# Graph attention layer on one NeuronCore: nodes laid out in 49 blocks of 128 where there were 50, node tables computed in 7 pieces of 7 blocks where there were 5 of 10

## The chip, the cores and the metric

The kernel runs on one core of one Trainium2 chip. The metric is the device time of one execution in microseconds. Three runs of the kernel before took 2503.68, 2481.40 and 2481.17 us; the median is 2481.4 us.

## The reference

6250 nodes with 64 features, 206,250 edges (100,000 random pairs in both directions, 200,000 in all, and one loop for each node), sorted by destination. For each edge the keys of its source, the queries of its destination and a projected edge feature are multiplied and summed in 4 heads of 16; the score is clipped to -5..5 and exponentiated, weighs the source's value row, and the messages are summed per destination. The sum is added to the node's features, and each row is normalized.

```
Kh = (x @ Wk.T + bk).reshape(n, H, D)
Qh = (x @ Wq.T + bq).reshape(n, H, D)
Vh = (x @ Wv.T + bv).reshape(n, H, D)
Ee = (edge_attr @ We.T + be).reshape(-1, H, D)
score = (Kh[src] * Qh[dst] * (1.0 / np.sqrt(D)) * Ee).sum(-1)
score = jnp.exp(jnp.clip(score, -5.0, 5.0))
msg = Vh[src] * score[..., None]
wV = jax.ops.segment_sum(msg, dst, num_segments=n)
out = _layernorm(x + wV.reshape(n, H * D))
```

## The kernel before

*Layout.* The nodes are padded to `NR = 128 * NB` rows, with `NB = 50`: 6400. Node n is row `n // NB` and block `n % NB` of a tile with 128 partitions. The edges are cut into 1612 tiles of 128 edges (`T`), eight tiles make a group (`G`), so there are 202 groups. Two groups make a step (the last steps have one); there are 105 steps.

*Start (before the main loop).* xT, with a row of ones, is loaded in `NB // CB` pieces of `CB = 10` blocks, by the ACT and SP queues in turn (L215, the ones by DVE in L216). For each piece the key and value rows of its blocks are computed by a matmul per block (L331), evicted two blocks at a time by ACT (L333), and written to the table `kv_tab` in HBM (L334). A second pass over the pieces does the queries (L361): ACT rounds them to bf16 (L363), DVE takes the remainder (L364), and a middle and a low part follow one pair of blocks later (L351 and L352, `rest_of_q`); each piece is written to `q3_tab` (L371) as three bf16 parts. Meanwhile POOL gathers the rows of x for the first 32 tiles (L238), and later, once `kv_tab` and the edges' sources `src_i` are there, the first key and value rows (L446). Last, the node features themselves are turned, split into three bf16 parts, and kept in SBUF as `parts`, one 128 x 192 tile for each of the `NB` blocks (L404 to L415).

*Where an edge gets its key and value row.* Of the 16 tiles of a step, 14 are gathered from `kv_tab` by POOL, one indirect DMA for each tile (L446). Five buffers of a step's size exist (`KVB`), and the gather for a later step waits until DVE's message (L617) has read the buffer. The other two tiles of most steps are *picked*: for a batch of 4 tiles (512 edges, two steps) the feature rows of the sources are made by one-hot matmuls over all node blocks. ACT computes `src - NB * row` (L493, `from`), DVE compares it with the block numbers (L503, `hots`), which gives for each block a 128 x 512 one-hot in bf16, and PE multiplies the block's `parts` with it: the high and middle parts (L514) and the low part (L519). When all blocks of a batch are summed, ACT copies the two results out (L526, L527), PE applies the key and value weights (L530 to L535, `picked_kv`), and ACT places the rows in the buffer (L541, `place_kv`).

*One batch in the main loop.* There are 47 such batches, and a batch spans four groups, g = 4m + i with i = 0 to 3. `CUTS` cuts the blocks into pieces of at most `MOST` blocks; a piece is one L503 instruction and one buffer of the pool `hot` (7 buffers). `PIECES` says which pieces go with which i. Before: 14 blocks in four pieces at i = 0, and 12 blocks in three pieces at i = 1, 2 and 3.

*Order in a group.* The program is written out by hand, engine by engine in this order: loads by SP (edges L175, queries L189, keys L554); DVE's products of this group (L600, L601, L604, L606); the first piece of the next group's one-hots (L503); DVE's add of a finished step (L644); the copies L526 and L527 (i = 0 alone); the picks of this group on PE (for i = 0 they stand after the following PE work); the edge projection for the next group (L435, onto a bias that ACT wrote in L564); the sums of a step (L630, 32 matmul passes, at every second group); the queries of the group after the next (L594); `picked_kv` (i = 0 and 2); on ACT the destination one-hots (L571, L577), `from` (L493), a widening copy (L625), `place_kv` (L541, i = 1 and 3), the bias (L564) and the exponential of the score (L610); DVE's message for the group before (L617); POOL's gathers; DVE's edge one-hots (L585); and the remaining pieces of the next group's one-hots (L503). Finished node blocks are closed, normalized and written out on the way (L658 to L679).

Of the kernel before, what the change touches and what calls it, by code (L numbers as in the profile page):

```python
# [7 lines left out]
F32 = mybir.dt.float32  # L8
BF16 = mybir.dt.bfloat16
I32 = mybir.dt.int32  # L10
AF = mybir.ActivationFunctionType
# [3 lines left out]
P = 128  # L15
N = 6250
C = 64
# [9 lines left out]
NR2 = 112  # L27
LG = 2
RG = 16
NB = 50  # L30
NR = P * NB
RING = 8
STEP = 31
# [1 line left out]
BATCHES = 16, 32, 47  # L35
KEYS = 26 * 8
W = 42
CB = 10
KVB = 5
XG = 4  # L40
TB = 4
# [21 lines left out]
AHEAD = 3  # L63
BATCH = 4
LAST = (NS - 8 - AHEAD) // 2
CUTS = 0, 4, 8, 12, 14, 18, 22, 26, 30, 34, 38, 42, 46, 50
MOST = 4
PIECES = (0, 1, 2, 3), (4, 5, 6), (7, 8, 9), (10, 11, 12)


def place_of(g):
# [36 lines left out]
def tile_gnn(ctx: ExitStack, tc: tile.TileContext, x, xT, wT, bias, beT, weT, eT, src, src_rows, dst,  # L108
             dst_rows, out):
    nc = tc.nc  # L110
    consts = ctx.enter_context(tc.tile_pool(name="consts", bufs=1))
    dram = ctx.enter_context(tc.tile_pool(name="dram", bufs=1, space=bass.MemoryType.DRAM))
# [1 line left out]


    kv_tab = dram.tile([NR, 2 * C], F32, name="kv_tab")
    q3_tab = dram.tile([NR, 3 * C], BF16, name="q3_tab")
    key_tab = dram.tile([NR2, 2 * G * P], BF16, name="key_tab")
    kv_v = kv_tab.rearrange("(p b) c -> p b c", p=P)
    q3_v = q3_tab.rearrange("(p b) (i c) -> p b i c", p=P, i=3)  # L120

    src_i = consts.tile([P, T], I32, name="src_i")
    dst_i = consts.tile([P, T], I32, name="dst_i")
# [37 lines left out]
    bkv_p = consts.tile([3, 2, 2 * C], BF16, name="bkv_p")  # L161
    parts = consts.tile([P, NB + 1, 3, C], BF16, name="parts")
    parts_flat = parts.rearrange("p b i c -> p (b i c)")
# [27 lines left out]
    with tc.tile_pool(name="nodes", bufs=1) as nodes, \  # L191
# [20 lines left out]
        rows_i = nodes.tile([NR2, 2, G * P], I32, name="rows_i")  # L212
        for i in range(NB // CB):
            s = slice(i * CB * P, (i + 1) * CB * P)
            (nc.scalar, nc.sync)[i % 2].dma_start(xT_sb[:C, s], xT[:, s])  # L215
# [41 lines left out]
        nc.vector.tensor_scalar(minus_row3, row3, -1.0, None, op0=OP.mult)  # L257
        nc.vector.tensor_scalar(minus_row50, row, -float(NB), None, op0=OP.mult)
        nc.vector.tensor_copy(row_b, row_i)
# [5 lines left out]
        def three_parts(out_, values, n, times):  # L265

            part = nodes.tile([3, n], BF16, name="part", bufs=2)
            mask = nodes.tile([3, 1], F32, name="mask", bufs=2)
            cut = nodes.tile([3, n], F32, name="cut", bufs=2)
            nc.vector.memset(cut, 0.0)  # L270
            for i in range(3):
                nc.vector.tensor_copy(part, values)
                nc.vector.tensor_scalar(mask, row[:3], float(i), None, op0=OP.is_equal)
                nc.vector.scalar_tensor_tensor(cut, part, mask, cut, op0=OP.mult, op1=OP.add)
                if i < 2:
                    nc.vector.tensor_sub(values, values, part)
            nc.vector.tensor_copy(out_, cut[:, None, :].to_broadcast([3, times, n]))

        def weights():
# [3 lines left out]
            nc.vector.tensor_scalar(bkv_sb[:, :C], bkv_sb[:, :C], 1.0 / D ** 0.5, None, op0=OP.mult)  # L283
            nc.vector.memset(parts[:, NB, 0], 0.0)

# [36 lines left out]

        q3 = nodes.tile([P, NB, 3, C], BF16, name="q3")
        for i in range(NB // CB):
            bs = slice(i * CB, (i + 1) * CB)
            kv_sb = chunks.tile([P, CB, 2 * C], F32, name="kv_sb")
            for b in range(0, CB, 2):
                ps = npsum.tile([P, 2, 2 * C], F32, name="ps")
                for u in range(2):
                    c0 = (i * CB + b + u) * P  # L330
                    nc.tensor.matmul(ps[:, u, :], xT_sb[:, c0:c0 + P], w_sb[:, :2 * C], start=True,  # L331
                                     stop=True)
                nc.scalar.activation(kv_sb[:, b:b + 2, :], ps, AF.Copy)  # L333
            nc.sync.dma_start(kv_v[:, bs, :], kv_sb)  # L334
            if i == 0:
                nc.sync.dma_start(rows_i, dst_rows)
# [10 lines left out]
        late = []  # L347

        def rest_of_q():
            q, two = late.pop(0)  # L350
            nc.scalar.activation(q3[:, two, 1], q, AF.Copy)  # L351
            nc.vector.tensor_sub(q3[:, two, 2], q, q3[:, two, 1])  # L352

        for i in range(NB // CB):
            for b in range(0, CB, 2):
                two = slice(i * CB + b, i * CB + b + 2)
                ps = npsum.tile([P, 2, 2 * C], F32, name="ps")
                q = ps[:, :, :C]
                for u in range(2):
                    c0 = (i * CB + b + u) * P  # L360
                    nc.tensor.matmul(q[:, u, :], xT_sb[:, c0:c0 + P], w_sb[:, 2 * C:], start=True,  # L361
                                     stop=True)
                nc.scalar.activation(q3[:, two, 0], q, AF.Copy)  # L363
                nc.vector.tensor_sub(q, q, q3[:, two, 0])  # L364
                late.append((q, two))
                if len(late) > 1:
                    rest_of_q()
            if late and b == CB - 2:
                rest_of_q()
            bs = slice(i * CB, (i + 1) * CB)  # L370
            nc.sync.dma_start(q3_v[:, bs], q3[:, bs])  # L371
        three_parts(be_p, be_sb, C, G)
        three_parts(bkv_p, bkv_sb, 2 * C, 2)
        masks()
# [82 lines left out]
    with tc.If(rv == 0) as branch:  # L457

        with tc.tile_pool(name="work", bufs=2) as work, \
# [3 lines left out]
            TO, OH, OF, PE, PQ, MSG, KB, SCORE, HOT, FROM, SRC = ({} for _ in range(11))  # L463
# [16 lines left out]
            def pairs(ap):  # L480

                return ap.rearrange("p (a b) -> p a b", b=2)
# [12 lines left out]
            def pieces(g):  # L495

                return [(g // 4, c) for c in PIECES[g % 4]] if 0 <= g < 4 * LAST else []

            def hots(m, c):
                lo, hi = CUTS[c], CUTS[c + 1]  # L500
                HOT[m, c] = work.tile([P, MOST, BATCH * P], BF16, name="hot", bufs=7)
                shape = [P, hi - lo, BATCH * P // 2, 2]
                nc.vector.tensor_tensor(  # L503
                    HOT[m, c][:, :hi - lo].rearrange("p b (a c) -> p b a c", c=2),
                    pairs(FROM[m])[:, None].to_broadcast(shape),
                    block2[:, lo:hi, None, :].to_broadcast(shape), op=OP.is_equal)

            def picks(todo):

                blocks = [(b, HOT[mc][:, b - CUTS[mc[1]], :]) for mc in todo  # L510
                          for b in range(CUTS[mc[1]], CUTS[mc[1] + 1])]
                for b, hot in blocks:
# [188 lines left out]
            for mc in pieces(0):  # L701
                hots(*mc)
            for g in range(NG + 1):
                now, before = g < NG, g > 0
                i, m = g % 4, g // 4
# [12 lines left out]
                for mc in ahead[:1]:  # L718
                    hots(*mc)
# [42 lines left out]
                for mc in ahead[1:]:  # L762
                    hots(*mc)
# [196 lines left out]
```

## Time and profile before

| what | value |
|---|---|
| runs | 2503.68, 2481.40, 2481.17 us; median 2481.4 us |
| profiled execution | 2496.53 us, its span 2494.6 us |
| granted TensorE clock, mean | 0.825 |
| PE busy | 1935.9 us (78%) in 12,299 matmul passes |
| DVE busy | 1494.2 us (60%) |
| POOL busy | 1350.8 us (54%), of it 1319.3 us in 1392 gathers |
| ACT busy | 908.6 us (36%) |
| picks, L514 and L519 | 583.8 + 306.1 us busy, 2350 matmuls each |
| one-hots, L503 | 697.2 us, 611 instructions |
| HBM | 218.74 MB read, 7.79 MB written |

Lines of the profile read as: line of the kernel, engine, operation, result <- operands, shapes, count; then busy time, mean duration, and the idle time of the engine just ahead of such instructions with what ended it ("issue" where the profile shows nothing that the engine waited for, "remote" where the releaser can't be told). PEld is the loading of weights. Timeline lines begin with the start and the duration in us from the start of the span.

### The profile page before, as it was taken

What the parts mean: (1) busy time and instruction counts of PE and PEld (TensorE: products, weight loads), DVE (VectorE), ACT (ScalarE), POOL (GpSimd) and SP (SyncE); (2) the same over time, 40 slices, a digit from 0 to 9 for tenths busy, and PEclk for the clock granted to TensorE, in tenths of its full rate; (3) what the DMA queues carried; (4) which work ended last, traced back from release to release, by engine and by line L of the source; (5) the groups of instructions that cost most, each with busy time, mean ns of one, the idle gap of its engine ahead of it and who ended that gap; (6) DMA issues with size and microseconds to landing.
All of it is one profiled execution on the core that took longest, in us unless ns stands there. A gap on an engine that the chain in (4) does not pass through costs nothing. (4 is left out here: it accounts for less than half of the span.)

```text
span 2494.6 us, 32642 instructions
## 1 busy us (share of the span) xinstructions
PE 1935.9 (78%) x12299; PEld 1331.1 (53%) x12299; DVE 1494.2 (60%) x2314; ACT 908.6 (36%) x1268; POOL 1350.8 (54%) x1434
## 2 busy tenths in 40 slices
PE   4477887887887887877778788788788778788875
PEld 4435555555555555455555555555555555455574
DVE  2356665665666666666556566566666666666653
ACT  1242433433442434233424234233343343342452
POOL 5435555555555555555555555555555555555551
PEclk9978888887887888788788788788888788888865
DMA  4332333333332333333323233233333332332341
GB/s 119 125 96 77 100 91 86 99 97 82 99 97 80 98 91 104 87 83 97 95 82 92 79 101 98 78 99 90 91 103 86 88 101 79 95 93 83 87 114 25
DMA packets 140877, 228.84 MB, mean 92 GB/s; under 512 B 71126, under 2 KB 71576, under 8 KB 140598
## 3 DMA queue, kind: packets, MB, share of 16 engines
q1 hardware_dynamic: 94758, 133.30, 18.3%
q0 software_dynamic: 45568, 92.37, 14.2%
q8 instruction: 98, 1.61, 0.3%
q10 hardware_dynamic: 384, 1.00, 0.2%
q14 instruction: 69, 0.57, 0.1%
HBM read 218.74 MB, written 7.79 MB: 91 GB/s over the span
## 5 line engine op out<-in xcount | busy, mean ns | idle before, releaser
L446 POOL DMA_INDIRECT kv<-kv_tab,src_i x1392 | 1319.3, 948 | 1086.1 <-DVE msg L617 642.3
L503 DVE TENSOR_TENSOR hot<-from,still 128x2048 bf16<-128x2048 bf16 (+1 forms) x611 | 697.2, 1173 | 156.9 <-PE low L519 117.0
L630 PE MATMUL room<-msg,off 128*128 128x64 f32 x3224 | 498.3, 298 | 284.8 <-issue 277.4
L630 PEld LDWEIGHTS room<-msg,off 128*128 128x128 f32 x3224 | 472.9, 220 | 304.3 <-issue 296.0
L514 PE MATMUL pick<-hot,parts 128*128 128x512 bf16 x2350 | 583.8, 401 | 9.3 <-issue 9.0
L541 ACT ACTIVATE kv<-room 128x256 f32<-128x256 f32 x94 | 36.2, 385 | 1379.0 <-PE room L630 511.8
L514 PEld LDWEIGHTS <-parts 128*128 128x128 bf16 x2350 | 235.7, 103 | 299.1 <-issue 88.7
L601 DVE TENSOR_TENSOR prod<-prod,pe 128x512 f32<-128x512 f32 x202 | 138.8, 687 | 418.4 <-remote 323.7
L435 PE MATMUL pe<-we_sb,et 128*128 128x128 f32 x1612 | 292.0, 331 | 110.5 <-ACT pe L564 68.9
L435 PEld LDWEIGHTS pe<-we_sb,et 128*128 128x128 f32 x1612 | 243.3, 229 | 182.7 <-ACT pe L564 88.9
L519 PE MATMUL low<-hot,parts 128*64 128x512 bf16 x2350 | 306.1, 386 | 14.5 <-issue 13.8
L577 ACT ACTIVATE to<-to,one_p 126x1024 bf16<-126x1024 bf16 x202 | 232.0, 1148 | 6.6
L571 ACT ACTIVATE to<-kb,minus_row 126x1024 bf16<-126x1024 bf16 x202 | 230.0, 1139 | 10.9 <-remote 5.5
L519 PEld LDWEIGHTS <-parts 128*64 128x64 bf16 x2350 | 120.3, 110 | 190.0 <-issue 114.8
L625 ACT ACTIVATE off<-of 128x2048 f32<-128x2048 bf16 (+2 forms) x105 | 191.9, 1828 | 52.5 <-remote 20.8
L644 DVE SCALAR_TENSOR_TENSOR acc<-room,above,acc 128x64 f32<-128x64 f32 x103 | 29.0, 282 | 243.2 <-ACT kv L541 177.9
L600 DVE TENSOR_TENSOR prod<-kv,pq 128x512 f32<-128x512 f32 x202 | 137.5, 681 | 25.2 <-remote 6.8
L594 PE MATMUL pq<-qw,to 126*128 126x64 bf16 x1612 | 109.7, 217 | 50.4 <-issue 40.2
L617 DVE TENSOR_TENSOR msg<-kv,score 128x512 f32<-128x512 f32 x202 | 138.7, 687 | 16.9 <-ACT score L610 12.7
L604 DVE TENSOR_REDUCE score<-prod 128x32 f32<-128x512 f32 x202 | 138.3, 685 | 6.9
L594 PEld LDWEIGHTS <-to 126*128 126x128 bf16 x1612 | 103.4, 120 | 61.1 <-issue 56.5
L585 DVE TENSOR_TENSOR of<-still,key 128x2048 bf16<-128x2048 bf16 (+2 forms) x105 | 123.3, 1175 | 0.2
(122 smaller groups left out, 1050.1 us busy)
## 6 DMA issues: line engine op xcount, KB each, us to landing
et<-in_eT SPq DMA_DIRECT2D x100, 512.0 KB
kb<-key_tab SPq DMA_DIRECT2D x201, 252.0 KB
kv<-kv_tab,src_i POOLq DMA_INDIRECT x1392
srcs<-in_src_rows SPq DMA_DIRECT2D x47, 256.0 KB
qw<-q_tab SPq DMA_DIRECT2D x202, 15.8 KB
kv_tab<-kv_sb SPq DMA_DIRECT2D x5, 640.0 KB
q_tab<-q SPq DMA_DIRECT2D x5, 480.0 KB
acc<-in_x SPq DMA_DIRECT2D x48, 32.0 KB
```

The costliest lines, as they stand in the source:

```text
L435: nc.tensor.matmul(pe[:, 2 * u:2 * u + 2, :], et[:, u, :], we_sb, start=False, stop=u == n // 2 - 1, skip_group_check=True)
L446: nc.gpsimd.indirect_dma_start(out=kv_of(g)[:, j, :], out_offset=None, in_=kv_tab[:, :], in_offset=bass.IndirectOffsetOnAxis(ap=src_i[:, t ...
L503: nc.vector.tensor_tensor(HOT[m, c][:, :hi - lo].rearrange("p b (a c) -> p b a c", c=2), pairs(FROM[m])[:, None].to_broadcast(shape), bloc ...
L514: nc.tensor.matmul(hi_mid, parts_flat[:, at:at + 2 * C], hot, start=b == 0, stop=b == NB - 1)
L519: nc.tensor.matmul(low[u * C:(u + 1) * C], parts_flat[:, at:at + C], hot, start=b < 2, stop=b >= NB - 2, skip_group_check=True)
L571: nc.scalar.activation(TO[g][:, :n, :], KB.pop(g)[:, :n * P].rearrange("p (j e) -> p j e", j=n), AF.Square, bias=minus_row3[:3 * W])
L577: nc.scalar.activation(TO[g][:, :n, :], TO[g][:, :n, :], AF.Relu, bias=one_p[:3 * W], scale=-1.0)
L594: nc.tensor.matmul(PQ[g][:, j, :], TO[g][:, j, :], QW[g], start=j == 0, stop=j == n - 1, skip_group_check=True)
L601: nc.vector.tensor_mul(prod[:, :n, :], prod[:, :n, :], PE[g][:, :n, :])
L617: nc.vector.tensor_mul(MSG[s][:, k:k + n, :].rearrange("p g (h d) -> p g h d", h=H), kv_of(g)[:, :n, C:].rearrange("p g (h d) -> p g h d", ...
L625: nc.scalar.activation(OF[s][:, :n, :], OH.pop(s)[:, :n, :], AF.Copy)
L630: nc.tensor.matmul(pa, OF[s][:, j, :], MSG[s][:, j, :], start=j == 0, stop=j == n - 1)
```

## The change

The nodes are laid out in 49 blocks (6272 rows). The tables are computed in 7 pieces of 7 blocks; since 7 is odd, each piece has three pairs of blocks and a single one, in both passes. A batch's blocks are cut into 12 pieces, eleven of 4 blocks and a last one of 5, three at each i; so the blocks at i = 0 to 3 are 12, 12, 12 and 13. The one-hot tiles hold 5 blocks each, and their pool has 6 buffers. A query window may reach beyond the last node, so `q3_tab` gets 64 more rows, which are filled by one more DMA.

```diff
-NB = 50
+NB = 49
-CB = 10
+CB = 7
-CUTS = 0, 4, 8, 12, 14, 18, 22, 26, 30, 34, 38, 42, 46, 50
-MOST = 4
-PIECES = (0, 1, 2, 3), (4, 5, 6), (7, 8, 9), (10, 11, 12)
+CUTS = 0, 4, 8, 12, 16, 20, 24, 28, 32, 36, 40, 44, 49
+MOST = 5
+PIECES = (0, 1, 2), (3, 4, 5), (6, 7, 8), (9, 10, 11)
...
-    q3_tab = dram.tile([NR, 3 * C], BF16, name="q3_tab")
+    q3_tab = dram.tile([NR + 64, 3 * C], BF16, name="q3_tab")
-    q3_v = q3_tab.rearrange("(p b) (i c) -> p b i c", p=P, i=3)
+    q3_v = q3_tab[:NR, :].rearrange("(p b) (i c) -> p b i c", p=P, i=3)
...
             for b in range(0, CB, 2):
-                ps = npsum.tile([P, 2, 2 * C], F32, name="ps")
-                for u in range(2):
+                n = min(2, CB - b)
+                ps = npsum.tile([P, 2, 2 * C], F32, name="ps")[:, :n]
+                for u in range(n):
...
-                nc.scalar.activation(kv_sb[:, b:b + 2, :], ps, AF.Copy)
+                nc.scalar.activation(kv_sb[:, b:b + n, :], ps, AF.Copy)
...
-                two = slice(i * CB + b, i * CB + b + 2)
+                n = min(2, CB - b)
+                two = slice(i * CB + b, i * CB + b + n)
                 ps = npsum.tile([P, 2, 2 * C], F32, name="ps")
-                q = ps[:, :, :C]
-                for u in range(2):
+                q = ps[:, :n, :C]
+                for u in range(n):
...
-            if late and b == CB - 2:
+            if late and b + 2 >= CB:
                 rest_of_q()
...
             nc.sync.dma_start(q3_v[:, bs], q3[:, bs])
+            if i == 0:
+                nc.sync.dma_start(q3_tab[NR:, :], q3[:64, 0].rearrange("p i c -> p (i c)"))
...
-                HOT[m, c] = work.tile([P, MOST, BATCH * P], BF16, name="hot", bufs=7)
+                HOT[m, c] = work.tile([P, MOST, BATCH * P], BF16, name="hot", bufs=6)
```

## The prediction

> **What bounds the kernel now.** I read the page first (who is busy), then the timelines of all engines through one batch, then a table of windows over the same batch, and last the start.
>
> ```profile
> PE 1935.9 (78%) x12299; PEld 1331.1 (53%) x12299; DVE 1494.2 (60%) x2314; ACT 908.6 (36%) x1268; POOL 1350.8 (54%) x1434
> L446 POOL DMA_INDIRECT kv<-kv_tab,src_i x1392 | 1319.3, 948 | 1086.1 <-DVE msg L617 642.3
> L514 PE MATMUL pick<-hot,parts 128*128 128x512 bf16 x2350 | 583.8, 401 | 9.3 <-issue 9.0
> L519 PE MATMUL low<-hot,parts 128*64 128x512 bf16 x2350 | 306.1, 386 | 14.5 <-issue 13.8
> ```
>
> No engine is full. The picks are the largest single work of PE, 583.8 + 306.1 = 890 us for 2350 blocks, 0.379 us a block. But 559 us of the span PE is idle, so the question is where in a batch that idle time lies. A batch (four groups, i = 0 to 3) is marked by the L526 copies: 47 of them from 188.3 to 2373.6, so 2185.3 / 46 = 47.5 us each. I take the batch from 1386.3 to 1433.96. Its windows (columns: busy time and count of PE, PEld, DVE, ACT, POOL, granted clock, DMA share, GB/s):
>
> ```profile
> 1386.30:1397.60 11.30, 11.26 (x60) 6.96 (x61) 6.86 (x11) 7.92 (x10) 5.67 (x6) 0.74 0.53 154
> 1397.60:1408.50 10.90, 10.90 (x87) 7.26 (x86) 8.02 (x12) 0.00 (x0) 7.75 (x8) 1.00 0.17 44
> 1408.50:1418.40 9.90, 9.56 (x72) 6.00 (x68) 8.89 (x15) 8.45 (x11) 5.98 (x7) 1.00 0.57 152
> 1418.40:1430.40 12.00, 3.76 (x15) 2.94 (x15) 3.75 (x5) 0.00 (x0) 7.26 (x8) 0.68 0.19 50
> 1430.40:1434.00 3.60, 3.04 (x20) 2.90 (x20) 3.16 (x6) 0.96 (x4) 0.00 (x0) 0.50 0.00 0
> ```
>
> PE is full for 32 us, then does 15 matmuls in 12 us, then works at half clock. The PE timeline says where:
>
> ```profile
> 1390.96 3.74 PE L514 MATMUL pick<-hot,parts 128*128 128x512 bf16 x14
> 1394.63 1.70 PE L519 MATMUL low<-hot,parts 128*64 128x512 bf16 x14
> 1396.26 2.76 PE L514 MATMUL pick<-hot,parts 128*128 128x512 bf16 x12
> 1398.96 1.49 PE L519 MATMUL low<-hot,parts 128*64 128x512 bf16 x12
> 1412.48 2.75 PE L514 MATMUL pick<-hot,parts 128*128 128x512 bf16 x12
> 1417.58 1.00 PE L630 MATMUL room<-msg,off 128*128 128x64 f32 x7
> 1426.86 0.27 PE L630 MATMUL room<-msg,off 128*128 128x64 f32 x1 [1.43 <-issue]
> 1430.42 2.58 PE L630 MATMUL room<-msg,off 128*128 128x64 f32 x11 [0.47 <-issue]
> ```
>
> After seven of the 32 sums of i = 3 the matmuls come one or two at a time, 0.7 us and its multiples apart, with no releaser ("issue"), until 1430.4. Beside it stands POOL, whose gathers come 1.25 us apart in runs of 6, 8 and 14 in this batch:
>
> ```profile
> 1398.58 1.13 POOL L446 DMA_INDIRECT kv<-kv_tab,src_i  x1 [3.48 <-DVE key_i L441]
> 1408.57 0.39 ACT L541 ACTIVATE kv<-room 128x256 f32<-128x256 f32 x1 [14.28 <-PE low L519]
> 1409.62 0.69 DVE L617 TENSOR_TENSOR msg<-kv,score 128x512 f32<-128x512 f32 x1 [0.16 <-issue]
> 1410.59 0.94 POOL L446 DMA_INDIRECT kv<-kv_tab,src_i  x1 [2.12 <-DVE msg L617]
> ```
>
> The run of 14 goes from 1410.59 to 1427.80, and the stall from 7.8 us after its start to 2.6 us after its end. Nearly every other long run does the same (first gap 7.8 to 10.6 us in); runs of 6 show none. ACT is held as well: L541 waits only for matmuls of groups before, yet starts at the end of the run of 8 (1398.58 to 1408.46). It lets the L564 bias, the exponential, the L617 message and so the run of 14 go. So a batch is PE's work plus a stall of some 12 us that POOL's runs place.
>
> **The change, part by part.** A block costs 2.76 / 12 + 1.49 / 12 = 0.354 us on a warm PE. The blocks of a batch go from 14, 12, 12, 12 to 12, 12, 12, 13.
>
> *Picks of i = 0, two blocks fewer:* -0.71 us. They lie before the runs of 8 and 14. PE next needs another engine at the edges L435 in i = 2 (1409.96), which need the ACT bias L564 that ended at 1409.45. If ACT stays where POOL's run puts it, PE can come at most 0.51 us earlier here, some 0.3 us in batches where L541 came later (L541 at 23.1 us of the batch in most, at 21.2 to 22.2 in others). Bounds 0 to 0.71; I take 0.5, the middle of the two caps and the whole.
>
> *Picks of i = 3, one block more:* +0.354 us. They lie in the 7.8 us before the stall, so three sums (0.11 us each) move behind it. At the half clock there they cost 0.22 each, so 0.35 to 0.66. I take 0.35: where the run of 14 and its stall begin 1.3 us earlier, batches are equally long (46.5, 46.9, 47.1 us against 46.3, 46.6, 47.3), so work pushed past the stall costs its own length.
>
> Net -0.15 us a batch (bounds -0.36 and +0.66), by 47: **-7 us** (-17 to +31).
>
> By the Trainium skill, "TensorE: Matmul & The Clock Gate", Part 1, the array runs at half rate after an idle window and is released after some 3.4 us of activity; were both removed blocks cold, i = 0 would be relieved of 1.06 us instead. The trace agrees on the gate (0.50 granted from 1430.4, 1.00 from 1397.6), and the 3.74 us for 14 against 2.76 for 12 shows the late ones warm, so the sum keeps 0.71.
>
> *Merged runs.* In 295.9, 1095.0, 1668.0, 1856.0 and 2142.7 (batch starts) L541 came before 21 us, the run of 8 ran into the next 6, and the batch took 48.6 to 49.2 us against about 46.8: +2.0 us. There the sums of i = 1 ended 4.6 to 5.1 us after the run of 8 began; in most others 6 to 7.3, in six 5.6 to 5.9. The run of 8 mostly begins at 11.7 to 11.8 us of the batch whether the lows of i = 0 ended at 9.0 or 10.5, so with fewer picks it stays, and the sums come up to 0.71 earlier: the six fall to about 5.0. Bounds 0 and 20 more merged batches (+40 us); I take four, **+8 us**.
>
> *One-hots:* per batch 13 L503 instructions (12 of 1.21 us, one of 0.68) become 12, the last 1.21 x 5/4 = 1.5 us: 0.4 us less DVE work. DVE idles 0.2 to 8 us ahead of its products for PE, which hides it: 0. The 0.3 us more stand before the L617 message of i = 3, needed at the seventh gather of the run (1418.09); it ended at 1417.55, so 0.5 us cover it; without cover 14 us in all, kept in the range. Six hot buffers instead of seven: a piece now reuses that of two groups before, whose lows precede on PE the edges that DVE's products wait for. Only i = 1 has no such cover, and there both versions wait for the same piece. 0.
>
> *Start.* 25 evictions of the kv table become 28, one block fewer; likewise for q (two ACT copies and two DVE subtractions each). While POOL gathers, ACT gets one through in some 9 us:
>
> ```profile
> 40.96 0.39 ACT L333 ACTIVATE kv_sb<-ps 128x256 f32<-128x256 f32 x1 [10.11 <-remote]
> 65.40 0.95 POOL L446 DMA_INDIRECT kv<-kv_tab,src_i  x1 [22.73 <-DMA src_i<-in_src]
> 106.18 0.28 ACT L363 ACTIVATE q<-ps 128x128 bf16<-128x128 f32 x1 [7.96 <-remote]
> ```
>
> The runs end at 42.7 and 102.6 either way. About five evictions pass in each; where a piece's odd block is among them, one or two blocks fewer are done, at 0.43 us a block afterwards, and each piece drains its pipe (0.2 us). **+2 us**, bounds 0 and 5. Two more kv writes, two more q writes and the 64 extra rows cost SP 0.3 to 0.7 us each before 113 us; it waits for ACT there, and the first gather waits for src_i. Xt pieces and memsets: 0.82 us instead of 1.12 each, seven instead of five, before ACT stalls anyway: 0.
> The Trainium skill speaks against smaller pieces ("DMA: Bandwidth & Descriptors", Anatomy of one DMA: some 2 us fixed per transfer, fitted on GpSimd's path). By that, five more would be 10 us if they stood in line; the first gather's wait for src_i and not for the table says they do not.
>
> Sum: -7 + 8 + 2 = +3 us on the profiled execution (2496.5 us, span 2494.6). It ran 15 us over the median of the runs, 2481.4; on that I forecast **2484 us**. A difference of about 1% (25 us) is what a measurement of this kernel can tell from no change.
>
> **The rivals.** *Nothing is lost* (chance 0.27): all of i = 0 passes, no batch merges. 47 x -0.354 + 2 = -15, 2467 us; if the stall also swallows the added block, 47 x -0.71 + 2 = -31, 2450. For: 0.379 us a block over 47 blocks is 18 us. Against: the run of 8 does not follow the lows.
> *Merging becomes the rule* (0.25): the sums of i = 1 end less than about 5.2 us after the run of 8 starts, L541 gets through, and the stall falls in i = 2. It decides from some 15 batches more: 15 x 2.0 - 7 + 2 = +25, 2506; with 25, 2526. For: one shift moves all batches alike. Against: most lie over a microsecond off, more than the 0.71.
> *The forecast* (0.48): gain and new merges cancel, 2470 to 2500.
>
> **The numbers.** Faster by over 1% needs the upper half of the first rival: 0.13. Slower by over 1% is the second beyond 15 batches, with the rare case of an uncovered message: 0.25. Within: 0.62. The range, 2450 to 2528, takes in both rivals and leaves out less than 2 in 10.
>
> **What would show it.** 2303 L514 and L519 matmuls, 564 one-hots, picks of 12, 12, 12, 13; the run of 8 still near 11.8 us of the batch; the stall still ending 2.6 us after the run of 14; five to twelve batches over 48.4 us; the q phase ending 1 to 3 us after 112. A batch mean under 46.9 or over 48 us would prove the steps on the batch wrong; a change in the first 146 us of over 5 us that on the start.

## The result and the profile after

The changed kernel took 2500.5 us (median of 13 runs, 2489.9 to 2520.3), the kernel before beside it 2486.8 us (13 runs, 2473.3 to 2503.7). The ratio of its runs to those of before is 1.0068, 95% interval 1.0041 to 1.0095: slower by 0.4 to 1.0%, inside what the prediction called no change. The profiled execution is the quickest of its 13 (2489.94 us, span 2488.1, granted clock 0.821), while that of before, at 2496.5, lies 10 us above its kernel's median. So the two profiles show what changed within a batch, and not the 13.7 us between the medians.

The page of the changed kernel, busy engines and the three groups that the prediction showed of before (lines moved by four: L450 gathers, L518 and L523 picks):

```profile
PE 1927.3 (77%) x12200; PEld 1320.4 (53%) x12200; DVE 1479.4 (59%) x2275; ACT 909.9 (37%) x1277; POOL 1350.5 (54%) x1434
...
L450 POOL DMA_INDIRECT kv<-kv_tab,src_i x1392 | 1319.0, 948 | 1081.2 <-DVE msg L621 637.9
...
L518 PE MATMUL pick<-hot,parts 128*128 128x512 bf16 x2303 | 578.8, 404 | 9.4 <-issue 8.9
...
L523 PE MATMUL low<-hot,parts 128*64 128x512 bf16 x2303 | 303.1, 386 | 15.9 <-issue 15.0
```

2303 blocks in place of 2350, and 8 us less busy PE in the picks; the span fell by 6.5 us from one profiled execution to the other.

An ordinary batch after the change, 1807.8 to 1855.1 us, in windows (columns as before: busy time and count of PE, PEld, DVE, ACT, POOL, granted clock, DMA share, GB/s):

```profile
1807.80:1819.50 11.70, 11.70 (x60) 7.14 (x61) 8.39 (x16) 7.88 (x10) 5.68 (x6) 0.74 0.51 157
1819.50:1832.00 12.50, 11.24 (x88) 7.13 (x86) 6.96 (x10) 1.00 (x4) 7.57 (x8) 1.00 0.17 46
1832.00:1844.30 12.30, 10.60 (x77) 7.27 (x77) 11.78 (x16) 7.46 (x9) 8.54 (x10) 1.00 0.54 139
1844.30:1855.10 10.80, 4.43 (x23) 4.19 (x23) 2.19 (x4) 0.93 (x4) 4.71 (x5) 0.51 0.14 37
```

and from the timeline of PE, with two lines of the other engines:

```profile
1812.41 3.48 PE L518 MATMUL pick<-hot,parts 128*128 128x512 bf16 x12
...
1817.24 2.76 PE L518 MATMUL pick<-hot,parts 128*128 128x512 bf16 x12
...
1826.10 2.75 PE L518 MATMUL pick<-hot,parts 128*128 128x512 bf16 x12
...
1831.00 0.39 ACT L545 ACTIVATE kv<-room 128x256 f32<-128x256 f32 x1 [15.26 <-PE low L523]
...
1833.02 0.95 POOL L450 DMA_INDIRECT kv<-kv_tab,src_i  x1 [3.73 <-DVE msg L621]
...
1834.46 2.97 PE L518 MATMUL pick<-hot,parts 128*128 128x512 bf16 x13
...
1839.98 1.86 PE L634 MATMUL room<-msg,off 128*128 128x64 f32 x14
...
1852.79 1.34 PE L634 MATMUL room<-msg,off 128*128 128x64 f32 x6 [0.92 <-issue]
```

The blocks are 12, 12, 12, 13. The picture is that of before: PE is full until some 9 us into the run of 14 gathers (1833.02 to 1850.23), then its sums come one at a time, with "issue" as the only reason, until 2.6 us after the run. The picks are shorter in front, and the stall stands where it stood.

A merged batch, 1758.9 to 1807.8 us, from the same timeline:

```profile
1771.54 0.94 POOL L450 DMA_INDIRECT kv<-kv_tab,src_i  x1 [3.07 <-DVE msg L621]
...
1772.32 3.68 PE L634 MATMUL room<-msg,off 128*128 128x64 f32 x32
...
1777.17 0.38 ACT L545 ACTIVATE kv<-room 128x256 f32<-128x256 f32 x1 [8.80 <-PE pick L518]
...
1793.66 4.53 PE L518 MATMUL pick<-hot,parts 128*128 128x512 bf16 x13
```

The sums of i = 1 end 4.5 us after the run of 8 began, L545 gets through on ACT, the next six gathers follow without a break to 1788.7, and PE's stall falls ahead of the last picks.

### The profile page after: what moved, and what is told of

Read it like the earlier page. It is cut to its first block, busy times and chain, and to the rows that moved or that the text cites. A ratio compares the mean times of both kernels' runs of the same rounds, so it can differ in the third digit from the quotient of the medians.

```text
span 2488.1 us, 32432 instructions
## 1 busy us (share of the span) xinstructions
PE 1927.3 (77%) x12200; PEld 1320.4 (53%) x12200; DVE 1479.4 (59%) x2275; ACT 909.9 (37%) x1277; POOL 1350.5 (54%) x1434
## 3 DMA queue, kind: packets, MB, share of 16 engines
q8 instruction: 98, 1.61, 0.3%
## 5 line engine op out<-in xcount | busy, mean ns | idle before, releaser
L450 POOL DMA_INDIRECT kv<-kv_tab,src_i x1392 | 1319.0, 948 | 1081.2 <-DVE msg L621 637.9
L507 DVE TENSOR_TENSOR hot<-from,still 128x2048 bf16<-128x2048 bf16 x564 | 681.6, 1236 | 150.9 <-PE low L523 106.5
L634 PE MATMUL room<-msg,off 128*128 128x64 f32 x3224 | 478.3, 297 | 220.4 <-issue 212.9
L518 PE MATMUL pick<-hot,parts 128*128 128x512 bf16 x2303 | 578.8, 404 | 9.4 <-issue 8.9
L634 PEld LDWEIGHTS room<-msg,off 128*128 128x128 f32 x3224 | 457.1, 218 | 236.3 <-issue 228.3
L545 ACT ACTIVATE kv<-room 128x256 f32<-128x256 f32 x94 | 36.2, 385 | 1376.4 <-remote 497.9
L439 PE MATMUL pe<-we_sb,et 128*128 128x128 f32 x1612 | 297.8, 334 | 139.7 <-ACT pe L568 101.6
L518 PEld LDWEIGHTS <-parts 128*128 128x128 bf16 x2303 | 233.0, 104 | 296.8 <-issue 93.9
L439 PEld LDWEIGHTS pe<-we_sb,et 128*128 128x128 f32 x1612 | 246.7, 230 | 214.9 <-ACT pe L568 120.7
L523 PE MATMUL low<-hot,parts 128*64 128x512 bf16 x2303 | 303.1, 386 | 15.9 <-issue 15.0
L523 PEld LDWEIGHTS <-parts 128*64 128x64 bf16 x2303 | 119.3, 110 | 190.2 <-issue 113.5
L598 PE MATMUL pq<-qw,to 126*128 126x64 bf16 x1612 | 117.3, 216 | 85.6 <-issue 74.1
```

The lines of the kernel that those rows point to most:

```text
L439: nc.tensor.matmul(pe[:, 2 * u:2 * u + 2, :], et[:, u, :], we_sb, start=False, stop=u == n // 2 - 1, skip_group_check=True)
L450: nc.gpsimd.indirect_dma_start(out=kv_of(g)[:, j, :], out_offset=None, in_=kv_tab[:, :], in_offset=bass.IndirectOffsetOnAxis(ap=src_i[:, t ...
L507: nc.vector.tensor_tensor(HOT[m, c][:, :hi - lo].rearrange("p b (a c) -> p b a c", c=2), pairs(FROM[m])[:, None].to_broadcast(shape), bloc ...
L518: nc.tensor.matmul(hi_mid, parts_flat[:, at:at + 2 * C], hot, start=b == 0, stop=b == NB - 1)
L523: nc.tensor.matmul(low[u * C:(u + 1) * C], parts_flat[:, at:at + C], hot, start=b < 2, stop=b >= NB - 2, skip_group_check=True)
L598: nc.tensor.matmul(PQ[g][:, j, :], TO[g][:, j, :], QW[g], start=j == 0, stop=j == n - 1, skip_group_check=True)
```

## The experiments

The runs were made on several chips, named here B to E; which chip the first comparison ran on is not known. The same kernel before takes very different times on them:

| chip | kernel before, us | kernels run there |
|---|---|---|
| of the first comparison | 2486.8 | the changed kernel: 1.0068 |
| B | 1827.2 | e1 to e4 |
| C | 2546.3 | f1 to f3 |
| D | 2551.3 | g1 to g3 |
| E | 2494.4 | h1, h2 |

All ratios below are to the kernel before on the same chip. Theory A is the prediction's: the batch is PE's work plus a stall that POOL's runs of gathers place; fewer picks at i = 0 gain a little and cause merged batches. Theory B: PE's amount of work counts, wherever it lies. Rival C: the start makes the difference.

**e1, start and layout alone.** The changed kernel with the old distribution; the 50th block of `parts` is zero.

```diff
+NBP = 50
-CUTS = 0, 4, 8, 12, 16, 20, 24, 28, 32, 36, 40, 44, 49
-MOST = 5
-PIECES = (0, 1, 2), (3, 4, 5), (6, 7, 8), (9, 10, 11)
+CUTS = 0, 4, 8, 12, 14, 18, 22, 26, 30, 34, 38, 42, 46, 50
+MOST = 4
+PIECES = (0, 1, 2, 3), (4, 5, 6), (7, 8, 9), (10, 11, 12)
...
-                HOT[m, c] = work.tile([P, MOST, BATCH * P], BF16, name="hot", bufs=6)
+                HOT[m, c] = work.tile([P, MOST, BATCH * P], BF16, name="hot", bufs=7)
...
```

> The changed kernel's layout and start (49 blocks, 7 pieces of 7, the 64 extra query rows), but in the main loop the blocks per i as before, 14, 12, 12, 12, in 13 pieces and with 7 hot buffers: a 50th block of picks is multiplied with a block of zero features. Theory A (the loss sits in the batches: fewer picks at i = 0 let the run of 8 gathers merge with the next 6 more often): as before, ratio 1.000 within 0.002, about five merged batches. Theory B (PE's amount of work counts, 0.354 us a block): as before too, 1.000. Rival C (the start, with its pieces of 7, is what costs): as the changed kernel, 1.005 to 1.008, 12 to 18 us more.

**e2, the old kernel with its two extra blocks at the end of the batch.**

```diff
-CUTS = 0, 4, 8, 12, 14, 18, 22, 26, 30, 34, 38, 42, 46, 50
-PIECES = (0, 1, 2, 3), (4, 5, 6), (7, 8, 9), (10, 11, 12)
+CUTS = 0, 4, 8, 12, 16, 20, 24, 28, 32, 36, 40, 44, 48, 50
+PIECES = (0, 1, 2), (3, 4, 5), (6, 7, 8), (9, 10, 11, 12)
```

> The kernel before (50 blocks, start in 5 pieces of 10) with the blocks per i as 12, 12, 12, 14 in place of 14, 12, 12, 12: the same instructions, two blocks' picks moved from i = 0 to i = 3. Theory A (picks missing at i = 0 are little gained and cause merged batches; picks added at i = 3 cost their length): 10 to 16 merged batches against 5, +8 x 1.4 = 11 us from these, and 47 x (0.7 - 0.5) = 9 us: ratio 1.006 to 1.010. Theory B (the amount of PE work counts, not its place): 1.000 within 0.002.

**e3, one block dropped.**

```diff
-CUTS = 0, 4, 8, 12, 16, 20, 24, 28, 32, 36, 40, 44, 49
+CUTS = 0, 4, 8, 12, 16, 20, 24, 28, 32, 36, 40, 44, 48
...
```

> The changed kernel without its 49th block of picks (its one-hot and its two matmuls are left out, so picked edges from that block get no row): 12, 12, 12, 12. Against the changed kernel this takes one block out of i = 3, against e1 two out of i = 0. Theory A: the i = 3 block gives back its length, 47 x 0.35 = 17 us against the changed kernel, and the merged batches stay at 10 to 16; against before 1.000 to 1.003, so two blocks less at i = 0 are worth nothing or less. Theory B (amount of work): 47 x 2 x 0.354 = 33 us less than before, 0.987.

**e4, the piece of five first.**

```diff
-CUTS = 0, 4, 8, 12, 16, 20, 24, 28, 32, 36, 40, 44, 49
+CUTS = 0, 5, 9, 13, 17, 21, 25, 29, 33, 37, 41, 45, 49
```

> The changed kernel with its piece of five blocks first and not last: 13, 12, 12, 12. The same instructions, one block's picks moved from i = 3 to i = 0. Theory A: merged batches fall to 6 to 10 and the sums of i = 3 come 0.35 us earlier: 10 to 20 us less than the changed kernel, ratio 0.998 to 1.002 to before. Theory B: as the changed kernel, whatever that is (1.007). Rival C (start): 1.007 too.

Measured: e1 1.0010 (0.9998 to 1.0023), e2 0.9968 (0.9955 to 0.9980), e3 1.0026 (1.0014 to 1.0039), e4 1.0008 (0.9996 to 1.0019). e1, e3 and e4 lie in theory A's ranges, but for another reason; e2 lies below those of both theories, and e3, with the least work, is the slowest. This chip shows no stall that anything could place. Three lines of e1's page (its line numbers are one further on):

```profile
PE 1678.9 (92%) x12294; PEld 1149.4 (63%) x12294; DVE 1491.2 (81%) x2322; ACT 909.0 (50%) x1277; POOL 1363.9 (74%) x1434
...
L451 POOL DMA_INDIRECT kv<-kv_tab,src_i x1392 | 1332.3, 957 | 433.0 <-issue 367.3
...
L635 PE MATMUL room<-msg,off 128*128 128x64 f32 x3224 | 395.2, 284 | 22.6 <-DVE acc L649 19.4
```

And one batch of e1 in windows, with the columns as above:

```profile
256.90:289.40 32.50, 31.78 (x246) 21.21 (x246) 29.17 (x43) 17.24 (x24) 24.57 (x27) 1.00 0.45 129
```

POOL's idle time of 433 us is 0.3 us after each of 1392 gathers: it issues without a pause, one per 1.25 us, and PE is full beside it. While POOL has a lead of filled buffers, the first batches run at PE's pace: 32.5 us in e1 with 50 blocks, 32.3 in e4 with 49, 31.9 in e3 with 48, so 0.3 us a block. But 28 gathers take 35 us, POOL's lead is used up (after about 880 us in e1, 740 in e3), and from there the gathers set the pace. The span ends 23.5 to 23.9 us after the last gather in all four. What differs is when that one is issued: after the first of them there is a single interval of over 2 us between two gathers, at about 97 us, of 9.9, 4.4, 9.2 and 7.3 us in e1 to e4; 50 to 70 other intervals are a little longer than 1.25 us, by 18.6, 12.5, 21.5 and 15.0 us in all; and the last gather comes at 1807.0, 1796.2, 1809.2 and 1800.7. On such a chip a block of picks is worth nothing: 50, 49 and 48 blocks (e1, e4, e3) took 1829.4, 1828.6 and 1831.9 us. Why e2 is quicker than the kernel before, whose start it has, stays open, since no profile of before was taken on this chip.

**f1, the changed kernel again** (no edit), on another chip.

> The changed kernel itself, since e1 to e4 and the kernel before beside them ran on another chip, at 1827 us and without PE's stalls: there POOL issued its gathers without a pause, 1392 of them 1.25 us apart = 1738 us. Theory A (the loss of 0.7% comes from PE's stalls, which the runs of gathers place): where the stalls are absent, the change does no more than its part at the start: 1.000 within 0.003, and where they are present, 1.004 to 1.010. Rival C (the start costs): 1.005 to 1.008 in both. Theory B (fewer blocks on a full PE): 0.990 without stalls.

**f2, the old kernel almost without gathers in the loop.**

```diff
-                if now and g == groups_of(step_of[g])[0] and step_of[g] + KVB - 1 < NS:
+                if now and g == groups_of(step_of[g])[0] and step_of[g] + KVB - 1 < min(NS, 2 * KVB):
```

> The kernel before with the main loop's gathers left out after the first ten steps (edges that need them then use rows of earlier steps); all else is there. If the runs of gathers cause PE's stalls: no stretch of 'issue' gaps in the batches, 33 to 36 us a batch, 1680 to 1800 us in all, on either chip; on a chip with stalls that is 690 us less. Rival (PE's stalls have another cause, its clock or its instructions): batches stay at 47 us on a chip with stalls. On a chip without stalls: if POOL is the bound there, 1690 to 1760 us; if PE is, 1820.

**f3, the old kernel with a pause until the gathers land.**

```diff
+            landed = accp.tile([1, 1], F32, name="landed")
             def gather(s):
                 for g in groups_of(s):
...
                             gather_kv(g, j)
+                            last = kv_of(g)[0:1, j, 0:1]
+                    nc.gpsimd.tensor_copy(landed, last)
```

> The kernel before, with POOL reading one element of the last gathered tile after the gathers of each group, so that it pauses until they have landed, some 2.6 us, four times a batch; no run of gathers is longer than 8. Theory A on a chip with stalls: the run of 14 is cut in two of 7 and the stall of some 12 us mostly goes: 38 to 46 us a batch, ratio 0.85 to 0.97. Rival (the stall depends on the number of gathers in flight or issued, not on the length of a run): 47.5 us a batch or more, 1.00 to 1.03. On a chip without stalls, where POOL is the bound, each pause counts: 186 x 2.0 to 2.6 us = 370 to 480 us, ratio 1.20 to 1.26.

Chip C has the stalls. f1: 0.9958 (0.9941 to 0.9975), the other sign than in the first comparison, and below the 1.004 to 1.010 that theory A gave for such a chip. Rival C, 1.005 to 1.008 on any chip, falls with it. f2: 1838.9 us against 2546.3 (one run). One line of its page:

```profile
L630 PE MATMUL room<-msg,off 128*128 128x64 f32 x3224 | 393.2, 282 | 14.0 <-issue 7.4
```

And a batch of f2 in windows:

```profile
1016.00:1048.50 32.50, 31.61 (x245) 21.22 (x247) 29.05 (x44) 17.26 (x24) 0.00 (x0) 1.00 0.26 76
```

Ahead of the sums PE is idle for 14 us where in the profile of before it was 284.8, and once the gathers stop, most batches take 32.5 us, just under the 33 to 36 expected. That is what PE's work comes to on a chip with stalls as on one without; the rest of the 47 to 48 us is due to the gathers, POOL's instructions and their transfers together, since f2 leaves out both. The 1839 us are above the 1680 to 1800 expected, for the start with its gathers is still there (first L526 copy at 190.9 us, 119.0 in e1).

f3: 0.9348 (0.9327 to 0.9368), within theory A's range. From its page:

```profile
L634 PE MATMUL room<-msg,off 128*128 128x64 f32 x3224 | 400.1, 284 | 48.7 <-DVE acc L648 35.1
...
L552 POOL COPY landed<-kv 1x1 f32<-1x1 f32 x194 | 34.4, 177 | 426.5 <-DMA kv<-kv_tab,src_i 426.5
```

The "issue" gaps ahead of the sums are nearly gone with the long runs (11.2 us in place of 277.4), though every gather is still made. The pauses cost 426.5 / 194 = 2.2 us each, and POOL now sets the pace, 44.2 us a batch. By the Trainium skill, "DMA: Bandwidth & Descriptors", Anatomy of one DMA, a transfer on GpSimd's path has a fixed cost of about 2.0 us, most of it the receipt of the last write; the 2.2 us, counted from the end of the gather's instruction, are near it, and the 3.1 us from its start are above it.

**g1, g2, g3: the change in three steps on one chip.** g1 is e1's kernel (start and layout), g2 is e3's (two blocks less at i = 0 than g1), g3 is the changed kernel (one block more at i = 3 than g2).

> The kernel of e1 again (start and layout of the changed kernel, blocks per i 14, 12, 12, 12 with a 50th block of zero features), for a chip with stalls. It is the first of three steps that lead from the kernel before to the changed one: start; two blocks less at i = 0 (g2); one block more at i = 3 (g3). Theory A (the start is worth nothing, the difference is made in the batches): ratio to before 1.000 within 0.002. Rival C (the start makes the difference): the ratio of g3, which was 1.0068 on one chip and 0.9958 on another. On a chip without stalls 1.001 as in e1.

> The kernel of e3 again (the changed kernel without its 49th block of picks, 12, 12, 12, 12; edges picked from that block get no row). Against g1, two blocks less at i = 0. My steps: 47 x 0.5 = 23 us less, given back by 5 to 10 more merged batches at 0 to 1.4 us: 0.990 to 0.997 of before. Theory A2 (the stall places itself, so blocks ahead of it are worth nothing): 1.000 within 0.003, with more merged batches. Theory B (every block counts 0.32 us, its step in the batches of e1, e3 and e4 that PE bounds): 47 x 0.65 = 31 us less, 0.988. On a chip without stalls 1.0026 as in e3.

> The changed kernel beside g1 and g2 on one chip: against g2 one block more at i = 3, in the stretch before the stall. My step: 47 x 0.354 = 17 us more than g2, 0.007. Theory A2: the sums that are pushed behind the stall cost their own length or double it at half clock, 0.35 to 0.66 a batch, 0.007 to 0.012 more than g2. Rival (the added block lies in the stall): as g2 within 0.002. Against before, with stalls, 0.995 to 1.008; without stalls, as e4, 1.001 within 0.002.

Measured on chip D, before 2551.3 us:

| kernel | median, us | ratio (95%) | step |
|---|---|---|---|
| g1 | 2546.7 | 0.9984 (0.9970 to 0.9998) | start: -4.6 |
| g2 | 2530.6 | 0.9929 (0.9904 to 0.9953) | two blocks less at i = 0: -16.1 |
| g3 | 2535.1 | 0.9945 (0.9925 to 0.9965) | one block more at i = 3: +4.5 |

By the scatter of the runs, the step at i = 0 is good to some 6 us, and that at i = 3 lies between -4 and +13. The step at i = 0 is within what the prediction's step gave, -23 us and a few merges. The block at i = 3 costs less than the 17 us expected, and its 4.5 us, 0.0016 of the time, can't be told from nothing: the rival, that it lies in the stall (within 0.002 of g2), fits, and my step and theory A2 do not. For g2 theory A2's 1.000 and theory B's 0.988 both lie outside the interval. Rival C falls again: the start is no loss. Times between the L526 copies of successive batches, by the runs that POOL made in them:

| chip, kernel | ordinary (6, 8, 14): number, mean us | merged (6, 14, 8): number, mean us |
|---|---|---|
| first, before | 33, 46.78 | 5, 48.82 |
| first, changed | 25, 46.71 | 13, 48.17 |
| C, f1 (changed) | 36, 47.94 | 4, 48.56 |
| D, g1 | 41, 48.45 | 1, 49.0 |
| D, g2 | 36, 47.94 | 5, 48.74 |
| D, g3 (changed) | 38, 48.07 | 3, 48.86 |

**h1 and h2, the changed kernel with two kinds of pause.** h1 has f3's edit, h2 this one:

```diff
+            idle = accp.tile([P, 512], BF16, name="idle")
             def gather(s):
                 for g in groups_of(s):
...
                             gather_kv(g, j)
+                    for _ in range(3):
+                        nc.gpsimd.memset(idle, 0.0)
```

> The changed kernel with the pause of f3: after the gathers of each group POOL reads an element of the last gathered tile, so it stops until they have landed. f3 brought 0.935 with 50 blocks; there POOL sets the pace, 28 x 1.25 us and four pauses of 2.2 us and some, 45 us for most batches. Theory A: with the stall mostly gone POOL is the bound and one block less is worth nothing more: 0.930 to 0.940 of before on a chip with stalls, so a version faster than both kernels. Theory B (each block counts on PE): 0.929 or less, 47 x 0.32 us under f3. On a chip without stalls 1.10 to 1.25, for each pause lengthens POOL's 35 us.

> The changed kernel with a shorter pause that waits for nothing: after the gathers of each group POOL clears a scratch tile of 128 x 512 three times, some 1 to 2 us, while the gathers are still under way. Theory A3 (what starves PE is that POOL issues gathers back to back; any pause lets PE refill): 28 x 1.25 + 4 x 1.5 = 41 us a batch, ratio 0.86 to 0.92 on a chip with stalls, better than h1. Rival (the gathers in flight must land first): the runs act as one, the stall stays, 47 to 50 us a batch, 0.98 to 1.03. On a chip without stalls 1.10 to 1.18.

h1: 2374.9 us, 0.9533 (0.9500 to 0.9567), outside the range I gave. Its time is 8 us under f3's, but chip E's kernel before is 52 us quicker than chip C's; the batch, 44.0 us, is f3's 44.2 within its scatter, as POOL's pace demands. h2: 2219.4 us, 0.8904 (0.8883 to 0.8926). POOL's timeline in h2:

```profile
1259.90 0.94 POOL L450 DMA_INDIRECT kv<-kv_tab,src_i  x1 [0.30 <-issue]
1260.84 1.71 POOL L556 MEMSET idle<- 128x512 bf16 x3
1262.73 0.95 POOL L450 DMA_INDIRECT kv<-kv_tab,src_i  x1 [0.17 <-DVE score L614]
```

1.7 us without a gather after every six or eight are enough for this gain. POOL is now never idle for long (467.8 us ahead of its gathers, 1081.2 in the profile of the changed kernel on the first chip), the batch is its 28 x 1.25 + 4 x 1.7 = 41.8 us (41.5 measured), and the kernel is 11% faster than the one before; the changed kernel was within 0.7% of that one on every chip where both ran.

The rival, that the gathers must land first, is not settled by it. In the trace of h2 the packets of a last gather end 1.3 us after its instruction (median), and the next gather starts 1.9 us after it, so in 135 of 176 pauses the transfer is over before POOL goes on. In the pause shown above, no packet moves in its last 0.6 us (columns as above, the last two are the DMA share and GB/s):

```profile
1262.10:1262.73 0.63, 0.63 (x13) 0.61 (x12) 0.59 (x3) 0.09 (x1) 0.46 (x2) 1.00 0.00 0
```

What h2 shows is that POOL need not wait for the signal of the landing. PE's stalls are not gone in it either: its idle time without a releaser is 3.6 us a batch (mean of the 5th to the 43rd), where the profile of the changed kernel has 7.4 and f3, with its longer pauses, 1.8; POOL's pace hides them. Whether a shorter pause would do, and what h2 costs on a chip like B, where POOL is the bound already, was not tried.

## Why the prediction was right or wrong, point by point

*What bounds the kernel: right, for the chips with stalls.* f2 shows that the gathers make the stall, and that it is larger than the "some 12 us" that I gave: 47.5 - 32.5 = 15 us a batch; beside the gap itself the clock is down (0.51 granted in the last window of the batch above, 0.74 in the first). f3 and h2 show that it shrinks when the runs are broken up.

*ACT held: a wrong reading.* I wrote that L541 waits only for matmuls of groups before. On chip B, in e1, each of the 94 copies (L546 there) starts 0.04 us after the 32 sums of its step have ended on PE, so it waits for these sums:

```profile
479.86 3.68 PE L635 MATMUL room<-msg,off 128*128 128x64 f32 x32
...
483.58 0.38 ACT L546 ACTIVATE kv<-room 128x256 f32<-128x256 f32 x1 [6.97 <-PE room L635]
```

In the batch that the prediction took, the same sums end at 1405.05, and L541 starts at 1408.57, 3.5 us later:

```profile
1401.37 3.68 PE L630 MATMUL room<-msg,off 128*128 128x64 f32 x32
```

In all of that profile 55 of the 94 sums end during a run of gathers, and 53 of their copies start 1.4 to 6.1 us late; of the other 39, 36 start within 0.1 us. So the signal that PE is done comes late during a run, and ACT waits for it. In h2 it is late still (over 1 us in 73 of the 83 that end during a run).

*Picks of i = 0: right.* I took 0.5 us a batch. In the ordinary batches of the first comparison the lows of i = 0 end 0.63 us earlier (9.92 to 9.29 us of the batch, means) and the edges of i = 2 come 0.44 us earlier (23.81 to 23.37). On chip D the ordinary batch is 48.45 - 47.94 = 0.51 us shorter. (The 1.06 us for two cold blocks was added up wrongly: at half rate they come to 2 x 0.71 = 1.42. No term used it.)

*Picks of i = 3: mis-sized.* I took 0.354 us a batch, the full length. D gives 0.13 (48.07 - 47.94), 4.5 us in all with an uncertainty of some 8. "If the stall also swallows the added block", which I kept for a rival, is nearer. In the first comparison the net is 46.71 - 46.78 = -0.07 us, near my -0.15; there it cannot be split.

*Merged batches: more than I took, by the profile.* I took four more at 2.0 us, +8; the profile after has eight more (13 against 5) at 48.17 - 46.71 = 1.5 us, +12. Part of why: I let L541 through if the sums of i = 1 end under 5.2 us after the run of 8 began. Counted to the end of the last sum, the merged batches of before lie at 4.9 to 5.4 (not 4.6 to 5.1), one ordinary batch at 5.1 and the others from 5.9 up; after, 12 of the 13 merged ones lie at 4.5 to 5.8, one at 6.5, and the ordinary ones from 5.5 up. So there is no sharp bound, and what else decides is open. On chips C and D ordinary batches begin at 4.9 to 5.2, and merges stay at three to five. There the gain on the ordinary batches remains, and the change is a gain.

*Start: near nothing, and its bound was wrong.* I took +2 us with bounds 0 and 5. The last q copies end at 113.3 us against 112.3, 1 us later as forecast, but the first edges L439 come at 144.5 us against 145.4, so -0.9 in the profiles. On D the step measured -4.6 (-0.5 to -7.7 by its interval), on B +0.1%, not clear of zero. I had no reason to exclude a gain. Where the 4.6 us come from stays open, since no profile of before was taken on D.

*One-hots and buffers.* 564 of L507 and 681.6 us busy, 15.6 less, hidden as forecast as far as the batches show; the buffer count was not tried by itself.

*The sum.* +3 us were forecast, on 2481.4. Thirteen runs put the kernel before at 2486.8, which is 5.4 of the 16.5 us between forecast and result. The other 11 us have no place in the profiles: from the one to the other the span fell by 6.5 us, with the additional merged batches in it. There the 38 ordinary and merged batches take 6.0 us more after the change, the eight batches of other kinds 10.8 us less, and the first L526 copy comes 1.8 us earlier. The profiled execution after is the quickest of its 13, and whether the slower ones merged more often is not known.

*What to look for.* The sign "five to twelve batches over 48.4 us" told nothing: the profile after has six, but that of before has ten.

*The rivals.* "Merging becomes the rule" did not come, though the first comparison went half way to it. "Nothing is lost" (47 x -0.354 + 2 = -15 us) is what C and D came to, 2531.9 - 2546.3 = -14.4 and -16.2 us, but in the number and not in its parts: on D these are -4.6, -16.1 and +4.5 where the rival has +2, -33 and +17. So the range held where the forecast was made, and in part by luck: the result lies at the upper end of the 2470 to 2500 that I took for most likely, and the terms at i = 3 and of the merges erred in opposite directions. The sign is not the change's own: it belongs to the change and the chip together. That the first chip's profile merges more than the others is seen in the table; why it does is open. That merging turns the sign is not shown, for the profile with 13 merged batches is itself quicker than that of before, and the first chip did not come again as such. The expectation of e2, 1.006 to 1.010 from moved blocks alone, could not be tested on B and was not tried elsewhere.

## What to carry to other kernels

When an engine stalls with no releaser in the profile, look for another engine that issues without a break beside it, and price work by whether it lies before, in or behind that stall: here two blocks less in front were worth 16 us, one more close to it 4.5, not clear of nothing. Try to break the run before trimming the work: three idle memsets after each group of gathers brought 11% on a chip with stalls, where a block of picks brought or cost half a percent. And measure a half percent on more than one chip, since the same change was 1.0068 on one and 0.9945 on another.

## What the runs showed of the hardware

The same program took 1827 us on one chip and 2487 to 2551 in four comparisons elsewhere, steady within each. On the quick one POOL's gathers (1.25 us each, as everywhere) leave PE alone; on the others PE nearly stops some 8 to 11 us into an unbroken run of gathers, and the signal that its sums are done reaches ACT 1.4 to 6.1 us late during a run (before, 53 of 55). Pauses of 1.7 us on POOL go with half of PE's idle time of this kind (3.6 us a batch against 7.4). Whether PE's own gaps come from the late signals, and what differs between the chips, was not found.

By the Trainium skill, "Runtime: NRT & Kernel Launch", Instruction fetch mechanics, each engine streams its instructions in blocks of 16 KiB over a DMA queue of its own, mostly hidden. The size agrees with one of the two instruction queues in the trace: q8 shows 98 packets and 1.61 MB, in the changed kernel's start on chip B (e1) and in the kernel before on the first chip alike; q14 has packets of 8 KiB. A failure of that hiding beside a run of gathers would look as these stalls do, but the trace of before speaks against it. In the stall from 1418.4 to 1430.4 q8 has no packet, and q14 this one:

```profile
q14 instruction: 1, 0.01, 0.3%
```

Of the 45 stalls beside runs of 14 in its main loop, 27 have a packet on neither queue from 1 us before PE's first gap to the last.
